# Router logits as one turned 128x256 block, and the stage lists of four phases in another order

## The chip, the cores and the metric

The kernel runs on one core of a Trainium2 chip. The metric is the time of one execution on the device in microseconds (us), given as the median of three runs. The engines are called PE or TensorE (matrix products and transposes), DVE or VectorE, ACT or ScalarE, POOL or GpSimd, and SP or SyncE, whose queue issues most of the transfers (DMAs). Each engine works through its own queue in order, and waits where an operand is not ready.

## The reference

The input is `x` of 32 sequences by 128 tokens by 128 features, with a context of the same shape. Two decoder layers follow each other, and each adds three parts to `x`: attention of 16 heads of 8 features, cross-attention to the context, and a mixture of 16 experts of which each token uses four. The routing of the first layer is

```python
scores = jax.nn.sigmoid(x2d @ router_weight.T)
sc = scores + e_bias[None, :]
group_scores = jnp.sum(jax.lax.top_k(sc.reshape(T, G, E // G), 2)[0], axis=-1)
_, gidx = jax.lax.top_k(group_scores, TG)
masked = jnp.where(smask > 0, sc, 0.0)
_, tidx = jax.lax.top_k(masked, K)
tw = jnp.take_along_axis(scores, tidx, axis=1)
```

and in the second layer the logits `x @ gate_w.T` are used without a sigmoid, with a softmax over the chosen four. The result per token is a row of 16 combine weights, zero for the experts not chosen; each expert's output is multiplied by its weight and summed.

## The kernel before

The 4096 tokens are 32 batches of 128; a group `g` is four batches (512 tokens, `GT`), and there are eight groups. A routing set `n` is two groups, eight batches (`NBR`), so each layer has four sets. Activations are kept per group in two forms: by token (`x[g]`, 128 tokens by 4 batches by 128 features) and, after normalisation (`xn`) and a turn on PE (`by_feature`, which transposes each batch), by feature (`hs[g]`, 128 features by 512 tokens), as matrix products need them.

**Routing.** `routing(n)` makes the logits of a set. For each of its eight batches one matmul takes the 128x128 block of `hs` as the stationary operand and the 16 router columns `W["r"]` as the moving one, so that token ends up on the partition: `lg` is 128 tokens by 8 batches by 16 experts in PSUM. A matmul in f32 is two records in the trace. `route` is a generator that turns the logits into combine weights, some steps at a time (`choose`, `chosen`): in the first layer it starts with a sigmoid on ACT (`route_groups`, with a load of ACT's tables before and after it), in the second with a copy on DVE (`route_softmax`, and `route` of the row tables). Routing happens eight times: set 0 of the first layer in `first_layers`, sets 1 to 3 in `mixture_layer`; three sets of the second layer in `second_layers`, the last (called n3) in `last_layer`.

**Send.** `send(n)` turns the combine weights to expert-by-token: eight transposes of 128x16 into `pct`, two ACT copies of 16x512 into slots of the ring `xn` (two buffers, shared with the normalised activations), and two DMAs into the DRAM tensors `combined`. Later `fetch` reads them back, each expert's row spread over 128 partitions (`share`). Send happens five times: four sets of the first layer and set 1 of the second.

**Gathered rows.** Sets 0, 2 and 3 of the second layer do not multiply all tokens with all experts. `placed` computes where each (token, choice) goes; `way_out` scatters rows into `rows_in` with 32 indirect DMAs on POOL per set; SP reads quads of four 128-row tiles (`rows_of`: one `rows` transfer, then four `row_weights`); PE multiplies them (`rows_turned`, `rows_up`, `rows_down`); `way_back` gathers the results with 32 indirect DMAs per set into `back` (three buffers), and `added` adds them to `x` on DVE.

**Order.** There are four phases: `first_layers` (0 to about 578 us: attention and cross-attention of layer one), `mixture_layer` (to about 798), `second_layers` (attention and cross-attention of layer two, to about 1062) and `last_layer`. Each is one call of `steps` with a list of stages. An entry `(stage, at, every, count, behind...)` runs the stage first at step `at` and then every `every` steps, `count` times. Within a step the stages of the list are written out in the order of the list; after each piece of one of them, one piece of a `between` stage is filled in, the first of the `between` list that still has pieces; what is left over is written at the end of the step. A stage named behind an entry waits in the list for that one. `first_layers` and `last_layer` are written by hand from the first step (`as_written=0`) and `second_layers` from step 8: there the order of the lists is the order in each engine's queue (in `last_layer` in SP's too). `mixture_layer` is left to the Tile scheduler, which takes the list as a priority.

In `first_layers` group `g`'s attention runs with four steps per group: `project` makes queries and keys with the rotary products, `turn` transposes them, `average` and `finish_` divide the weighted sums and apply the output projection (DVE `aT`, PE `proj`). `biased` adds the output bias to `x` on POOL. `second_layers` does the same with feature maps (`totals` makes `pS` and `fsums`, `finish` the projection).

## Time and profile before

| | |
|---|---|
| median of three runs | 1350.46 us (1350.32 to 1351.31) |
| the profiled execution | 1348.26 us, of which the span is 1346.2 us |
| mean granted clock of PE | 0.971 |
| instructions | 27567 |
| PE busy | 1236.1 us (92%) |
| DVE, ACT, POOL busy | 857.6, 581.2, 531.4 us |
| `logits` on PE | 128 records, 11.3 + 3.8 us |
| `pct` on PE, its copy on ACT | 40 records, 5.3 us; 10 copies of 16x512, 5.5 us |
| HBM traffic | 99.34 MB read, 27.85 MB written |

A row of a timeline has the start in us, the length in us, the engine, the line of the kernel, the operation, the output and input tiles with their shapes, the number of records, and in brackets the idle time before it with what ended it. A row of stretches has, for each stretch, its length, then the busy time and number of instructions of PE, of PE's weight load, of DVE, ACT and POOL, then the granted clock of PE (1.00 is full), the mean busy share of the DMA engines and GB/s. In the view of slices each digit is the busy share of one fortieth of the span in tenths. Records of PE overlap: the step from one start to the next is what one occupies.

### The profile page before, as it was taken

How to read it: one execution, taken by the hardware profiler on the slowest of the kernel's cores; microseconds unless marked ns; L12 is line 12 of the kernel's file. 1: busy time of each engine (PE TensorE's matmuls, PEld its weight loads, DVE VectorE, ACT ScalarE, POOL GpSimd, SP SyncE). 2: the span in 40 equal slices, each digit the busy share in tenths (PEclk: the TensorE clock that was granted, in tenths of full speed). 3: DMA queues.
4: the chain of work that ended last, by engine and by line, in shares of the span. 5: the costliest groups of instructions: out<-in, count | busy, mean ns of one | idle time of the engine just before them, and what ended most of it. 6: DMA issues, size and time to landing. Idle time of an engine off the chain costs nothing. (4 is left out here: it accounts for less than half of the span.)

```text
span 1346.2 us, 27567 instructions
## 1 busy us (share of the span) xinstructions
PE 1236.1 (92%) x10753; PEld 835.9 (62%) x10753; DVE 857.6 (64%) x2295; ACT 581.2 (43%) x856; POOL 531.4 (39%) x715
## 2 busy tenths in 40 slices
PE   7689999999999999699999989999987889989995
PEld 6357767777777777544344446666664457767753
DVE  5746867677768675376866536787877575225463
ACT  4445445454555433232332234665654424433331
POOL 6244243445351222132100015455527653746654
PEclk9789999999999999899999999999998899999998
DMA  9401321121211111363262320000000488999933
GB/s 327 126 1 33 101 65 34 33 51 31 50 29 37 34 33 33 75 145 85 43 127 61 66 100 2 2 2 2 2 2 25 144 256 272 306 296 287 305 120 93
DMA packets 89673, 129.07 MB, mean 96 GB/s; under 512 B 9888, under 2 KB 63776, under 8 KB 88128
## 3 DMA queue, kind: packets, MB, share of 16 engines
q1 hardware_dynamic: 76768, 102.59, 27.2%
q0 software_dynamic: 6144, 12.60, 3.0%
q10 hardware_dynamic: 6624, 12.05, 2.4%
q8 instruction: 87, 1.43, 0.4%
q14 instruction: 50, 0.41, 0.1%
HBM read 99.34 MB, written 27.85 MB: 94 GB/s over the span
## 5 line engine op out<-in xcount | busy, mean ns | idle before, releaser
L1307 ACT ACTIVATE e<-scores 128x1024 f32<-128x1024 f32 x128 | 124.1, 1021 | 67.3 <-PE scores L977 67.2
L977 PE MATMUL y<-sg,wide 128*128 128x512 f32 x224 | 119.3, 621 | 15.1 <-DVE sg L2268 8.0
L2245 POOL DMA_INDIRECT back<-rows_out,place x96 | 91.2, 950 | 58.7 <-DVE x L2256 31.1
L1145 POOL TENSOR_SCALAR xn<-x,mv,r 128x128 f32<-128x128 f32 x78 | 67.4, 870 | 91.3 <-PE pxn L1154 82.7
L1927 ACT ACTIVATE sg<-pg 128x512 f32<-128x512 f32 x72 | 43.0, 597 | 118.9 <-PE pg L977 110.0
L1561 ACT ACTIVATE e<-xscores 128x1024 f32<-128x1024 f32 x64 | 62.0, 1021 | 67.7 <-PE xscores L977 67.7
L1322 DVE STREAM_TRANSPOSE by_token<-sums 128x512 f32<-128x512 f32 x64 | 45.3, 707 | 71.0 <-PE sums L977 70.9
L1928 DVE TENSOR_TENSOR sg<-sg,pu 128x512 f32<-128x512 f32 x72 | 49.3, 685 | 60.7 <-PE pu L977 58.1
L1116 POOL TENSOR_SCALAR r<-mv 128x4 f32<-128x4 f32 x46 | 13.2, 286 | 189.2 <-DVE mv L1135 189.2
L977 PE MATMUL scores<-qb,k 32*128 32x512 f32 x512 | 75.2, 658 | 13.4 <-ACT e L1307 7.0
L1116 POOL TENSOR_SCALAR r2x<-mv 128x2 f32<-128x2 f32 x16 | 3.8, 235 | 195.3 <-DVE mv L1135 195.3
L977 PE MATMUL pg<-hx,wide 128*128 128x512 f32 x152 | 78.0, 595 | 0.0
L977 PEld LDWEIGHTS y<-sg,wide 128*128 128x128 f32 x224 | 36.6, 191 | 66.3 <-DVE sg L1930 36.3
L977 PE MATMUL pu<-hx,wide 128*128 128x512 f32 x152 | 77.7, 593 | 0.0
L977 PE MATMUL sums<-e,v 128*32 128x128 f32 x2048 | 72.7, 284 | 0.7 <-ACT e L1307 0.7
L977 PE MATMUL po<-e,v 128*64 128x128 f32 x1024 | 66.2, 280 | 4.3 <-DVE v L1575 4.2
L2230 DVE TENSOR_TENSOR sgrows<-sgrows,pu 128x512 f32<-128x512 f32 x36 | 24.7, 687 | 70.6 <-PE pu L977 61.2
L977 PEld LDWEIGHTS sums<-e,v 128*32 128x32 f32 x2048 | 56.7, 113 | 19.3 <-issue 4.9
L1609 ACT COPY av<-po 128x512 f32<-128x512 f32 x64 | 37.6, 587 | 71.2 <-PE po L977 70.4
L977 PE MATMUL po<-av,wide 128*128 128x256 f32 x256 | 60.0, 388 | 7.7 <-DVE av L1629 7.7
L977 PE MATMUL pqk<-h,wide 128*128 128x256 f32 x256 | 64.4, 397 | 1.1 <-ACT h L1157 1.1
L977 PEld LDWEIGHTS po<-e,v 128*64 128x64 f32 x1024 | 56.4, 139 | 12.8 <-issue 7.4
(326 smaller groups left out, 2974.0 us busy)
## 6 DMA issues: line engine op xcount, KB each, us to landing
row_weights<-in_w1f_dram SPq DMA_DIRECT2D x144, 192.0 KB, 4.0
factor<-factors SPq DMA_DIRECT2D x64, 256.0 KB, 4.4
share<-combined SPq DMA_DIRECT2D x32, 512.0 KB, 14.2
rows_in<-in_few SPq DMA_DIRECT2D x36, 256.0 KB, 4.2
rows<-rows_in SPq DMA_DIRECT2D x36, 256.0 KB, 4.0
rows_out<-yrows ACTq DMA_DIRECT2D x36, 256.0 KB, 4.5
share<-combined SPq DMA_DIRECT2D x8, 1024.0 KB, 5.4
wide<-in_w1f_dram SPq DMA_DIRECT2D x1, 3272.0 KB
```

What stands on the lines that cost most here:

```text
L977: last[0] = nc.tensor.matmul(*args, **kw)
L1116: nc.gpsimd.tensor_scalar(t, src, add, None, ALU.add)
L1145: eng.tensor_scalar(n[:, b, :], x[g][:, b, :], mv[:, b, 0:1], r[:, b : b + 1], ALU.subtract, ALU.mult)
L1307: nc.scalar.activation(e[-1], ps[:, bass.ts(n, 2)].rearrange("p c i s -> p (c i) s"), AF.Exp, scale=scale)
L1322: nc.vector.transpose(tt.rearrange("p i t r -> p (i t r)"), po.rearrange("p i s -> p (i s)"))
L1561: nc.scalar.activation(e[-1], ps[:, n].rearrange("p r c s -> p (r c) s"), AF.Exp, scale=scale)
L1609: nc.scalar.copy(avs[w][n][:, :, bass.ts(b, S)], po)
L1927: nc.scalar.activation(sg, pg, AF.Silu)
L1928: nc.vector.tensor_tensor(sg, sg, pu, ALU.mult)
L2230: nc.vector.tensor_tensor(sg, sg, pu, ALU.mult)
L2245: nc.gpsimd.indirect_dma_start(out=outs[n, u][:, k], out_offset=None, in_=rows_out[n], in_offset=bass.IndirectOffsetOnAxis(ap=places[n][:, ...
```

## The change

`logits` replaces the matmuls of all four routings. The stationary operand is now 32 columns wide (the 16 router columns and the 16 that lie next to them in the weight tile, whose results are not read), and each of four matmuls has 256 tokens as the moving operand and writes to one quarter of the 128 PSUM partitions. ACT copies the 128x256 result to SBUF, into a slot of the ring `xn` (in `last_layer` of a tile `turned`), and two 128x128 transposes on PE bring the tokens back to the partitions. The reader takes them in another order through `by_chunk`. `send` transposes a set's 128x128 combine weights at once, copies them in one ACT instruction, and stores each half with a DMA of 64 rows of 512 bytes. In all four phases the entries of the stage lists are permuted, and some start at another step.

```diff
...
+    def wider(self, name, n):
+a = self.spans[name][0]
+return self.tile[:, a : a + n]
+
...
     (weights, 4, 1, NU),
-    (lambda k: xvalues(2 * k), (5, 12), 2, EARLY - 1),
     (lambda w: xproject("k", w + EARLY), 8 + 2 * EARLY, 2, NW - EARLY),
+    (lambda k: xvalues(2 * k), (5, 12), 2, EARLY - 1),
     (lambda k: xvalues(2 * k + 1), 11, 2, NW),
     (xfinish_a, 13, 2, NW),
-    (lambda g: average(g * GB + GB + 3), 12, 4, NG - 1),
     (turn_in, (1, 3, 9), 4, NG, scaled),
+    (lambda g: average(g * GB + GB + 3), 12, 4, NG - 1),
     (xturn, (8, 13), 4, NG, xscaled),
     (xweights, (9, 11), 1, NU),
+    of_four(average, 0, 5),
     (finish_, 12, 4, NG - 1),
...
     of_four(average, 2, 7),
-    of_four(average, 0, 5),
     (lambda _: average(3), 7, 1, 1),
     of_four(average, 1, 6),
-    (finish_first, 7, 1, 1),
     [
...
     (first(routing), 29, 1, 1),
+    (first(send), 39, 1, 1, choose),
     (turn, (3, 7, 11), 4, NG, head_norms),
-    (head_squares, (2, 5, 10), 4, NG, head_means),
-    (first(send), 40, 1, 1, choose),
+    (finish_first, 7, 1, 1),
     (xfinish_b, 13, 2, NW),
+    (head_squares, (2, 5, 10), 4, NG, head_means),
     (xaverage, (9, 11), 1, NU),
...
         (xfinish_c, 14, 2, NW),
+        (norms, (0, 1, 8, 12), 4, NG),
         (head_means, (2, 5, 10), 4, NG),
...
         (xscaled, (8, 13), 4, NG),
-        (norms, (0, 1, 8, 12), 4, NG),
         (xnorm, (7, 12), 4, NG, finish_first, finish_),
-        (biased, 3, 4, NG),
-        (lambda _: choose(0, 5), 30, 1, 11),
+        (biased, 1, 4, NG),
         (xnormalize, 12, 2, NW, xweights),
         (rnorm_, 22, 4, NBR // GB),
-        (filled, 15, 1, 12),
         (rscaled_, 23, 4, NBR // GB),
+        (lambda _: load_w0f(), 21, 1, 1),
         (lambda k: load_late(LATE[k]), (17, 18), 1, len(LATE)),
-        (lambda _: load_w0f(), 20, 1, 1),
+        (filled, 16, 1, 12),
+        (lambda _: choose(0, 5), 30, 1, 11),
     ],
...
+    def by_chunk(s):
+
+return s.rearrange("p (c j) e -> p c j e", j=2)
+
+    def logits(wk, r, sources, name):
+
+
+pl = sm([128, 2 * S], "logits")
+for c, rows in enumerate(quarters):
+    mm(pl[rows], lhsT=r, rhs=sources[c // 2][:, bass.ts(c % 2, 2 * S)], start=True, stop=True)
+t = wk.tile([128, GT], F32, name=name, bufs=2)[:, 0 : 2 * S]
+nc.scalar.copy(t, pl)
+pt = sm([128, 2, S], "plogits")
+for j in range(2):
+    nc.tensor.transpose(pt[:, j], t[:, bass.ts(j, S)], ident)
+return pt.rearrange("p j (c e) -> p c j e", c=4)[:, :, :, 0:E]
+
     def route_groups(lg, wk):
...
 s = wk.tile([128, NBR, E], F32, name="s", bufs=1)
-nc.scalar.activation(s, lg, AF.Sigmoid)
+nc.scalar.activation(by_chunk(s), lg, AF.Sigmoid)
 yield
...
 s = wk.tile([128, NBR, E], F32, name="s", bufs=1)
-nc.vector.tensor_copy(s, lg)
+nc.vector.tensor_copy(by_chunk(s), lg)
 yield
...
 def routing(wk, n):
-    lg = sm([128, NBR, E], "logits")
-    for i, g in enumerate(groups(n)):
-        for b in range(GB):
-            mm(lg[:, i * GB + b, :], lhsT=hs[g][:, bass.ts(b, S)], rhs=W["r"], start=True, stop=True)
+    lg = logits(wk, W.wider("r", 32), [hs[g] for g in groups(n)], "xn")
     choices[n] = route(lg, n)
...
     comb = combs.pop(n)
+    pt = sm([128, S], "pct")
+    nc.tensor.transpose(pt, comb.rearrange("p b e -> p (b e)"), ident)
+    cT = wk.tile([128, GT], F32, name="xn", bufs=2)[:, 0:S]
+    nc.scalar.copy(cT, pt)
     for i, g in enumerate(groups(n)):
-        pt = sm([E, GB, S], "pct")
-        for b in range(GB):
-            nc.tensor.transpose(pt[:, b, :], comb[:, i * GB + b, :], ident)
-        cT = wk.tile([E, GT], F32, name="xn", bufs=2)
-        nc.scalar.copy(cT, pt.rearrange("p b s -> p (b s)"))
         weights[g] = dram.tile([E, GT], F32, name="combined")
-        nc.sync.dma_start(out=weights[g], in_=cT)
+        dst = bass.AP(weights[g].tensor, weights[g].offset, [[S, GB], [GT, E], [1, S]])
+        nc.sync.dma_start(out=dst, in_=cT[bass.ts(i, GB * E), :])
...
+also = [(lambda k, more=stage: more(wk, k), *when) for stage, *when in more]
 steps(
-    (fetch, 0, 1, 1),
-    (lambda _: fetch(1), 0, 1, 1),
+    (lambda n: groups(norm, scaled)(n + 2), 3, 4, NR - 2),
+    also[0],
+    also[3],
+    also[5],
     (lambda _: groups(norm, scaled)(1), 0, 1, 1),
     (lambda _: groups(turn)(1), 0, 1, 1),
-    (lambda n: groups(norm, scaled)(n + 2), 3, 4, NR - 2),
     (lambda n: routing(n + 1), 0, 4, NR - 1),
-    (lambda n: stages[4](n + 1), 0, 4, NR - 1),
+    also[4],
     (lambda n: groups(turn)(n + 2), 3, 4, NR - 2),
     (lambda n: send(n + 1), 3, 4, NR - 1),
+    (lambda n: stages[4](n + 1), 0, 4, NR - 1),
+    (lambda _: fetch(1), 2, 1, 1),
     (lambda n: fetch(2 * n + 2), 3, 4, NR - 1),
-    (lambda n: fetch(2 * n + 3), 4, 4, NR - 1),
-    *((lambda k, more=stage: more(wk, k), *when) for stage, *when in more),
+    (lambda n: fetch(2 * n + 3), 3, 4, NR - 1),
+    (fetch, 0, 1, 1),
+    also[1],
     (experts, 0, 1, 2 * NG),
+    also[2],
 )
...
     s = edge.tile([128, NBR, E], F32, name="s", bufs=1)
-    nc.vector.tensor_copy(s, lg)
+    nc.vector.tensor_copy(by_chunk(s), lg)
     yield
...
 def routing(n):
-    lg = sm([128, NBR, E], "logits")
-    for i, g in enumerate(of_set(n)):
-        for b in range(GB):
-            mm(lg[:, i * GB + b, :], lhsT=hs[g][:, bass.ts(b, S)], rhs=W["r"], start=True, stop=True)
+    lg = logits(wk, W.wider("r", 32), [hs[g] for g in of_set(n)], "turned")
     choices[n] = tables.route(lg, n)
...
 steps(
-    fetch_at(5, 6),
     fetch_at(0, 0),
+    fetch_at(4, 3),
     fetch_at(1, 0),
+    fetch_at(5, 6),
     fetch_at(2, 0),
-    fetch_at(4, 3),
-    fetch_at(6, 9),
     (several(each(rows_of, quads), (0, 1)), 0, 1, 1),
-    fetch_at(3, 0),
-    (several(turn, of_set(n3)), 6, 1, 1),
     once(tables.owned, n2, 3),
+    (several(turn, of_set(n3)), 6, 1, 1),
+    fetch_at(3, 0),
+    fetch_at(6, 9),
     (each(rows_turned, quads), Q, 1, NQ),
-    once(routing, n3, 6),
     (ups, 0, 1, LAST),
...
     (each(rows_up, quads), Q, 1, NQ),
-    fetch_at(7, 16),
     once(tables.owned, n3, 12),
+    once(routing, n3, 6),
+    fetch_at(7, 16),
     (downs, 0, 1, LAST),
...
     between=[
-        once(several(norm, of_set(n3)), None, 3),
+        (each(added, batches(0)), 23, 1, NBR),
         once(tables.placed, n2, 1),
-        once(chosen, n3, 7),
-        (each(added, batches(n2)), 33, 1, NBR),
+        (each(added, batches(n3)), 42, 2, NBR),
+        once(several(norm, of_set(n3)), None, 3),
         (each(rows_of, quads[2:]), Q, 1, NQ - 2),
-        (each(tables.way_out, to_send(n2, 2)), 2, 1, 4),
-        (each(way_back, batches(n3)), 40, 2, NBR),
+        once(chosen, n3, 7),
         once(tables.placed, n3, 9),
-        once(chosen, n2, 0),
+        (each(tables.way_out, to_send(n3, 1)), 9, 1, NBR),
+        (each(tables.way_out, to_send(n2, 2)), 1, 1, 4),
         (each(way_back, batches(n2)), 29, 1, NBR),
+        once(chosen, n2, 0),
+        (each(added, batches(n2)), 32, 1, NBR),
+        (each(way_back, batches(n3)), END + 1, 2, NBR),
         once(several(scaled, of_set(n3)), None, 4),
-        (each(added, batches(0)), 24, 1, NBR),
         (each(way_back, batches(0)), 19, 1, NBR),
-        (each(tables.way_out, to_send(n3, 1)), 10, 1, NBR),
-        (each(added, batches(n3)), END + 4, 2, NBR),
     ],
...
 steps(
+    (finish, 9, 4, NG),
     (features_q, 3, 4, NG),
...
     (later(project), 5, 4, NG - 1),
-    (finish, 9, 4, NG),
+    (xvalues, 11, 4, NG),
     (later(turn), 6, 4, NG - 1),
     (lambda _: send(early, 1), 43, 1, 1),
-    of_four(xweights, 2, 14),
     of_four(xweights, 1, 13),
-    (first(rturn), 20, 4, 3 * R),
-    (xvalues, 11, 4, NG),
+    of_four(xweights, 2, 14),
+    (later(turn_in), 4, 4, NG - 1),
     of_four(xweights, 3, 15),
-    (xkey, 10, 4, NG),
     (xturn, 11, 4, NG, xscaled),
-    (later(turn_in), 4, 4, NG - 1),
+    (first(rturn), 20, 4, 3 * R),
+    (xkey, 10, 4, NG),
     (average, 5, 1, NU),
...
     (xaverage, 13, 1, NU),
-    (xfinish, 17, 4, NG),
-    (xproject, 11, 4, NG),
     (first(routing), (25, 33, 42), 1, 3),
     of_four(xweights, 0, 12),
+    (xfinish, 17, 4, NG),
+    (xproject, 11, 4, NG),
     between=[
+        (norm_, 0, 4, NG - 1),
         (xscaled, 11, 4, NG),
+        (lambda _: choose(1, 3), 34, 1, 6),
+        (first(rscaled), 19, 4, 3 * R, xturn),
+        (scaled_, 3, 4, NG - 1),
         (placed, 33, 1, 1),
-        (lambda _: choose(1, 3), 35, 1, 6),
-        (lambda i: tables.way_out(0, to_send[3 * i : 3 * i + 3]), 36, 1, 11),
         (xnorm, 10, 4, NG),
-        (lambda _: choose(0, 3), 26, 1, 6),
-        (first(rscaled), 19, 4, 3 * R, xturn),
-        (norm_, 0, 4, NG - 1),
+        (lambda _: choose(0, 3), 27, 1, 6),
+        (lambda i: tables.way_out(0, to_send[3 * i : 3 * i + 3]), 37, 1, 11),
         (first(rnorm), 18, 4, 3 * R),
-        (scaled_, 3, 4, NG - 1),
     ],
...
         mixture0,
-        ((l1_setup, 10, 1, 1), *((lambda _, k, i=i: stages[i](k), 11 + i, 1, 1) for i in range(5))),
+        ((l1_setup, 10, 1, 1), *((lambda _, k, i=i: stages[i](k), at, 1, 1) for i, at in enumerate((10, 10, 12, 14, 16)))),
     )
```

## The prediction, made before the changed kernel ran

> **What bounds the kernel now.** I read the page's busy times and slices first, to see which engine is full and where; then the same by stretches of time; then the timeline of TensorE around each place that the change touches.
>
> ```profile
> PE 1236.1 (92%) x10753; PEld 835.9 (62%) x10753; DVE 857.6 (64%) x2295; ACT 581.2 (43%) x856; POOL 531.4 (39%) x715
> ...
> PE   7689999999999999699999989999987889989995
> ...
> DMA  9401321121211111363262320000000488999933
> ```
>
> TensorE works 92% of the span, and the digits below 9 are where it waits: the start, about 540 to 580, about 1000 to 1060, and the last layer. The stretches say the same in us:
>
> ```profile
> 200.00:525.00 325.00, 323.43 (x3609) 248.18 (x3608) 239.79 (x609) 155.63 (x219) 115.72 (x164) 1.00 0.16 38
> ...
> 600.00:780.00 180.00, 177.76 (x483) 76.92 (x482) 116.77 (x289) 52.72 (x88) 15.82 (x20) 1.00 0.35 72
> 800.00:1000.00 200.00, 191.17 (x2590) 133.30 (x2582) 147.70 (x432) 119.05 (x166) 93.99 (x141) 1.00 0.03 13
> ...
> 1062.00:1300.00 238.00, 215.53 (x1266) 161.59 (x1267) 117.41 (x295) 89.14 (x148) 137.50 (x143) 0.96 0.85 274
> 1300.00:1346.00 46.00, 32.27 (x113) 17.75 (x111) 18.13 (x43) 9.48 (x16) 25.63 (x28) 0.90 0.28 82
> ```
>
> The first column after the length is TensorE. From 200 to 525 and from 600 to 780 it is the bound at full clock (1.00): what it no longer does there comes off the span. From 1062 on the DMA share (0.85) stands beside it, and after 1300 the end hangs on POOL's gathers. The places themselves:
>
> ```profile
> 389.00 1.03 PE L977 MATMUL pqk<-h,wide 128*128 128x256 f32 x4
> ...
> 392.02 1.85 PE L977 MATMUL logits<-wide,hx 128*128 128x16 f32 x16
> 393.72 0.69 PE L977 MATMUL proj<-wide,o 128*128 128x128 f32 x4
> 394.35 1.08 PE L977 MATMUL xsums<-e,ones_by 128*32 128x128 f32 x32
> 395.36 0.88 PE L977 MATMUL po<-e,v 128*64 128x128 f32 x12
> ```
> ```profile
> 543.28 1.04 PE L1894 MATMUL pct<-in_few,comb 128*16 128x128 f32 x8
> 544.60 1.08 PE L977 MATMUL xsums<-e,ones_by 128*32 128x128 f32 x32 [0.28 <-ACT xn L1896]
> 548.27 3.76 PE L977 MATMUL po<-e,v 128*64 128x128 f32 x32 [2.60 <-DVE v L1575]
> ```
> ```profile
> 577.98 0.71 PE L977 MATMUL proj<-wide,o 128*128 128x128 f32 x4 [0.53 <-ACT o L1644]
> ```
>
> From one start to the next, 16 logits records hold TensorE 1.70 us (392.02 to 393.72).
>
> **Routing (8 times).** Removed: 1.70 us. Added on TensorE: four matmuls of 256 columns into four column quarters, two records each, and two transposes. The trace has no quarter matmul of 256 columns. Bounds: 32 quarter records of 128 columns take 1.01 us (394.35 to 395.36), so eight of twice the width take 0.50; run one after another they cost as the full-width 256-column records do, (389.86-389.00)/4 = 0.215 each, 1.72. I take 0.50, since the nearest row has the same shape of stationary tile and differs only in width. Transposes: eight take about 1.0 us here (the pct rows, and eight pxn in 1.04), so two 0.25. New total 0.75, serial 1.97.
> The Trainium skill ("TensorE: Matmul & The Clock Gate", section "Why this matters for your kernels") gives 2.38x for three column tiles where the row above shows more than three-fold overlap (32 records in 1.01 us, against about 0.12 each for the transposes); by it the four matmuls would be an estimated 0.72 us, and eight routings 1.8 us dearer than I count.
>
> Between the two halves now stands a ScalarE copy of 128x256. The nearest row is the 384 ns ScalarE pass over 128x256, which stopped TensorE 0.53 us at 577.98. Where the transposes follow the logits directly (first layers, second layers, last layer) I charge 0.53, at least 0 and at most one exponential of 1.02 more. In the mixture layer the scheduler puts another 512-column matmul (0.86 us from start to start) in between, which covers 0.53; without that cover 1.6 us come back over three routings. The sigmoid or copy after it reads the same 128x128 values in another order; its 0.28 to 0.29 us are off TensorE's path. The copy lies in ScalarE's idle time (52.72 busy of 180).
> The Trainium skill ("TensorEngine Tiling (Array Packing)", "PSUM Bottleneck") speaks against the change here: tiling quickens TensorE but not the copy out of PSUM, which can become the limit; by it all eight would stall, 1.6 us more than I count.
> So a routing saves 1.70-0.75 = 0.95 covered, 0.42 stalled.
>
> **Send (5 times).** Eight transposes (543.28 to 544.60 less the wait of 0.28: 1.04; 0.96 at 1054.99) become one, 0.12: saves 0.84 where TensorE is full. Two ScalarE copies of 574 ns become one (128x128 rows: 267 ns). The two DMAs stay two, 64 rows of 512 B instead of 16 of 2 KB, 32 KB each; SyncE's queue is otherwise in the same order but for one send that moves ahead of one factor transfer, two issues of about 0.5 us in a queue that idles there.
>
> **Stage by stage.**
> First layers, start. The turn of group 0 moves ahead of the output projection, where TensorE waited 3.26 and 0.76 us for DVE's aT (61.49, 63.04), so the scores come up to 3.5 us sooner; but the next chain (x, its norm, POOL's and ScalarE's parts, then pqk at 72.19) runs through the same projection. POOL's bias add (1.27 us) moves ahead of the rotary adds: at the start it may delay them by 1.27, later it falls into POOL's idle 6.3 to 7.6 us before them. Range -3.5 to +1.3; I take -0.5, the part of ScalarE's work that certainly leaves that chain. Routing(0) at 392: -0.42. The send at 543: 0, because TensorE then waits 2.60 for VectorE's v, behind a factor transfer that does not move; what is late next is the same transfer. The stop of 7.29 us at 571.26 for a factor is as it was.
>
> Mixture layer (TensorE 177.76 of 180): three routings 2.85, three sends 2.52. At its end TensorE stands 0.85 (795.06, VectorE's sg) with a 512-column matmul behind it that now goes before: -0.85. Eight transposes of rotated keys (0.86) leave the full stretch for a place where TensorE idled 0.78; their two ScalarE copies and a POOL pass then end about when the next stage needs them: -0.7 to +1, I take -0.35. The other moves here (fetches, the second layer's first stages at steps 10, 10, 12, 14, 16) permute work inside the full stretch, and SyncE's queue keeps its order: 0. Sum -6.6 (-4 to -8.5).
>
> Second layers. Routing -0.42. The output projection moves ahead of pS and qkv (3.6 us sooner). It needs aT (reciprocal 0.96, multiply 0.29). In the first group that ends at 823.9 and TensorE arrives at 822.5: +1.4. In four later groups (847, 875, 904, 933) aT is there 0.4 to 0.6 us before the new slot: 0. VectorE: an add (0.28) and four Max passes (0.41) move ahead of a norm that TensorE already waits 1.90 for: +0.7. Near 1034, where TensorE waits 3.62 for VectorE's norm, two statistics passes go into earlier idle time: -0.8. POOL's scatter of set 0 starts a step later, so three calls (1.26 apart) no longer stand before the context norm, for which TensorE waited 0.18, 1.10 and 0.33: at most -1.6, I take -0.65, less than half, since the exponentials stop it 2.12 soon after. Last routing and send at 1053: the copies are shorter, -0.85. The second routing lies before a wait of 2.02 for VectorE: 0. Sum -0.6 (-4 to +4).
>
> Last layer. Those three scatter calls are made up at the end, where 8 calls in a row become 11:
>
> ```profile
> 1072.33 0.95 POOL L2138 DMA_INDIRECT rows_in<-wide,place  x1 [0.30 <-issue]
> ```
> ```profile
> 1074.57 0.32 SPq L2195 DMA_DIRECT2D rows<-rows_in  x1
> 1075.65 2.89 SPq L2209 DMA_DIRECT2D row_weights<-in_w1f_dram  x4
> ```
> ```profile
> 1087.83 1.05 PE L977 MATMUL pg<-hrows,row_weights 128*128 128x128 f32 x8
> ```
>
> Set 0 is scattered about 4 us later (3 x 1.26), SyncE's first row transfer waits for it, and all its weight transfers queue behind. Landing 6.9 us after issue (median there), the first weights come at 1078.5+6.9+4 = 1089.4 against a need at 1087.8; from 1094.76 on the queue waits for free buffers anyway. Range 0 to +4, I take +1. Routing(n3) -0.42; its VectorE copy comes one chunk later, but the placement keeps its place in VectorE's order, so the 4.54 wait for set n3's rows at 1186.40 stays. The adds of returned rows move one or two steps earlier. The end does not hang on them: the last quad's results (pyrows 1289.43, out at 1291.24) release 32 POOL gathers, 1294.15 to 1333.9, and TensorE idles 7.99 us for those. 0.
>
> Sum: -0.5 -0.42 -6.6 -0.6 -0.42 +1.0 = -7.5. The profiled execution took 1348.26 (span 1346.2, 2.06 around it), 2.2 under the median of 1350.46. From its own time 1340.8; on the scale of the medians **1343**.
>
> **Rivals.**
> Only half: quarters run serially. A routing then costs 1.97, or 2.50 with the stall: 3 x -0.27 and 3 x -0.80 turn my +4.1 of routings into -3.2, about 7.3 worse: 1350, no change. For it: the 512-column rows at full width show no overlap. Against: the 32 quarter records in 1.01.
> More: the start passes on its 3.5 and the second layers their 4: -7.5-3.0-3.4, 1336.6. For it: both waits stand in the trace. Against: each has a second chain at nearly the same time.
> Slower: the moved projection. It has only about 0.5 us of slack to aT in the later groups, and pS, qkv and all behind stand in TensorE's queue. If VectorE (147.70 busy of 200) reaches the reciprocal some 2 us later than before, TensorE waits 1.5 us in each of the other seven groups, +10.5, and the sum is +3: 1353.5. It decides at about 1.5 us of lateness. For it: VectorE is backlogged around 1000. Against: in most groups it waited 0.2 to 1.6 us for fsums, so it is on time.
>
> **How the numbers follow.** Two medians of this kernel tell apart about 0.2%, 2.7 us. Forecast (-3 to -11) 0.58, more 0.14, half or none 0.12, slower 0.16 (the projection 0.10, the late weights with an uncovered copy 0.06). Faster 0.72, same 0.12, slower 0.16. The range drops about 1 in 10 on each side: from the "more" case, 1336, to the slower one, 1353; the forecast's own is 1339 to 1347.
>
> **What would show it.** Right: PE busy lower by about 11 us; four quarter logits matmuls within 0.6 us; 600 to 780 still full with the mixture's end about 7 us sooner; rows<-rows_in of set 0 no more than 4 us later against the end of the second layers. Wrong: quarter records 0.2 us apart one by one; aT waits in the later groups; TensorE waiting for row_weights near 1085 to 1100.

## The result, and the profile after

The changed kernel took 1344.17 us (median of 11 executions, 1338.39 to 1348.84); the kernel before, on the same chip and between them, 1354.32 us (11 executions, 1347.78 to 1359.7). The ratio is 0.9928, with a 95% interval of 0.9903 to 0.9952: 9.8 us less, between 6.5 and 13.1. The forecast was a gain of 7.5 us, and its time 1343.0. Two slow executions of the kernel before, 1465.17 us at a granted clock of 0.832 and 1365.74 us, are left out of every comparison below.

The two profiles shown are further from this than the kernels are. The profiled execution of the changed kernel took 1345.81 us (span 1344.0), 2.45 us less than that of the kernel before; but that of before, with 1348.26, lies some 6 us under the median of its own executions, and its granted clock of 0.971 is above their mean. So below I read places and waits from the pair of profiles, and totals from the medians.

From the page of the changed kernel, its busy times and the slices:

```profile
PE 1225.4 (91%) x10670; PEld 821.1 (61%) x10670; DVE 853.2 (63%) x2295; ACT 580.1 (43%) x859; POOL 531.8 (40%) x715
...
PE   7689999999999999689999989999987789989995
...
PEclk9889999999999999789999999999989899989997
DMA  9401322111111111363253220000000378999933
```

TensorE is busy 10.7 us less (1236.1 before), close to the 11 that were announced, and its slices keep their shape. Of the stretches, in the columns explained with the profile before, those that answer to the ones shown there:

```profile
200.00:525.00 325.00, 322.74 (x3545) 247.10 (x3546) 234.94 (x600) 155.02 (x218) 109.79 (x159) 1.00 0.15 38
...
600.00:780.00 180.00, 177.82 (x458) 74.28 (x457) 120.50 (x298) 52.13 (x89) 16.38 (x21) 1.00 0.34 72
...
800.00:1000.00 200.00, 189.04 (x2559) 129.65 (x2551) 147.54 (x430) 117.48 (x165) 94.08 (x141) 0.99 0.01 3
...
1062.00:1300.00 238.00, 215.35 (x1269) 160.22 (x1270) 120.65 (x302) 90.64 (x151) 144.76 (x150) 0.97 0.84 276
1300.00:1344.00 44.00, 28.55 (x104) 16.11 (x102) 15.27 (x38) 8.28 (x14) 23.98 (x25) 0.82 0.28 83
```

The mixture layer (600 to 780) is as full as before: what left TensorE there was followed by other work at once. From 800 to 1000 TensorE is busy 2.1 us less in the same 200 us, with waits that were not there. Where the mixture layer ends, from its last matmul to the second layer's first positive keys (pkphi), before and then in the changed kernel:

```profile
795.06 1.12 PE L977 MATMUL y<-sg,wide 128*128 128x512 f32 x2 [0.85 <-DVE sg L1928]
796.92 0.66 PE L1945 MATMUL pyt<-in_few,y 128*128 128x128 f32 x4 [0.73 <-ACT y L1942]
...
803.01 0.50 PE L977 MATMUL pkphi<-feat,y 32*128 32x128 f32 x8 [1.66 <-ACT qphi L2468]
```
```profile
789.18 2.11 PE L981 MATMUL y<-sg,wide 128*128 128x512 f32 x4
792.02 0.66 PE L1963 MATMUL pyt<-in_few,y 128*128 128x128 f32 x4 [0.73 <-ACT y L1960]
...
799.45 0.50 PE L981 MATMUL pkphi<-feat,y 32*128 32x128 f32 x8 [1.65 <-ACT qphi L2489]
```

The wait of 0.85 us is gone, and from the last turned result (pyt) to the first positive keys it is 7.43 us instead of 6.09.

The new operations on TensorE's timeline, one routing of the first layers, one of the mixture layer and one send:

```profile
386.86 0.64 PE L981 MATMUL logits<-hx,wide 128*32 128x256 f32 x8
388.04 0.44 PE L1779 MATMUL plogits<-in_few,xn 128*128 128x128 f32 x2 [0.54 <-ACT xn L1776]
388.31 0.61 PE L981 MATMUL proj<-wide,o 128*128 128x128 f32 x4
...
621.60 0.27 PE L1910 MATMUL pct<-in_few,comb 128*128 128x128 f32 x1
621.71 1.02 PE L981 MATMUL pg<-hx,wide 128*128 128x512 f32 x2
...
637.43 0.64 PE L981 MATMUL logits<-hx,wide 128*32 128x256 f32 x8
638.00 1.13 PE L981 MATMUL pg<-hx,wide 128*128 128x512 f32 x2
638.96 0.38 PE L1779 MATMUL plogits<-in_few,xn 128*128 128x128 f32 x2
639.18 1.02 PE L981 MATMUL pu<-hx,wide 128*128 128x512 f32 x2
```

Eight quarter records occupy TensorE 0.57 us from start to start (637.43 to 638.00), the two turns 0.22 to 0.27, a send's turn 0.11. In the mixture layer the 512-column matmul at 638.00 stands between the halves and there is no wait; at 388.04 TensorE waits 0.54 us for the ScalarE copy. Where a factor ends the first layers:

```profile
543.28 1.84 PE L981 MATMUL po<-e,v 128*64 128x128 f32 x16 [3.71 <-DVE v L1579]
546.32 1.98 PE L981 MATMUL po<-e,v 128*64 128x128 f32 x16 [1.20 <-DVE v L1579]
...
568.72 3.78 PE L981 MATMUL po<-av,wide 128*128 128x256 f32 x8 [7.48 <-DVE av L1633]
573.80 3.78 PE L981 MATMUL po<-av,wide 128*128 128x256 f32 x8 [1.30 <-DVE av L1633]
...
578.12 0.71 PE L981 MATMUL proj<-wide,o 128*128 128x128 f32 x4 [0.53 <-ACT o L1648]
```

The wait for VectorE's v, 2.60 us before, is 4.91 now in two parts. The eight records at 573.80 ran at a granted clock of 0.50; those of before took 1.99 us at a clock of 1.00:

```profile
575.45 1.99 PE L977 MATMUL po<-av,wide 128*128 128x256 f32 x8 [0.41 <-DVE av L1629]
```

And the last layer's first rows and weights, on the queue of SyncE and on TensorE:

```profile
1079.57 0.32 SPq L2216 DMA_DIRECT2D rows<-rows_in  x1
1080.66 2.89 SPq L2230 DMA_DIRECT2D row_weights<-in_w1f_dram  x4
```
```profile
1089.20 1.05 PE L981 MATMUL pg<-hrows,row_weights 128*128 128x128 f32 x8
```

The rows go out 5.0 us later than before, their weights too, and TensorE starts the first matmul with them 1.37 later (1087.83 before) and shows no wait for weights: it does the layer's own matmuls meanwhile.

### The profile page after: what moved, and what is told of

The parts are those of the page before. It is cut to its first block, busy times and chain, and to the rows that moved or that the text cites. A ratio compares the mean times of both kernels' runs of the same rounds, so it can differ in the third digit from the quotient of the medians.

```text
span 1344.0 us, 27393 instructions
## 1 busy us (share of the span) xinstructions
PE 1225.4 (91%) x10670; PEld 821.1 (61%) x10670; DVE 853.2 (63%) x2295; ACT 580.1 (43%) x859; POOL 531.8 (40%) x715
## 4 chain that ended last, share of the span: by engine, by line
PE 63%; DVE 14%; DMA 8%; POOL 5%; ACT 4%; issue 3%; SPq 1%; POOLq 0%; DVEq 0%; ACTq 0%
PE pqk L981 7%; PE po L981 7%; PE pg L981 6%; PE pu L981 6%; PE y L981 5%; PE scores L981 4%; PE xscores L981 4%; PE pval L981 3%; PE sums L981 3%; DMA factor<-factors 3%; DMA row_weights<-in_w1f_dram 2%; PE proj L981 2%; PE pyrows L981 2%; POOL back L2266 2%; PE pS L981 2%
```

## The experiments

Theory A at the start: the cheaper logits and sends carry the gain by the price of each removed record, and the stage lists together give nothing. Against it: the lists carry the gain, or part of it, with the second rival that some of the lists give back what others win. To hold kernels against each other I use, beside the ratios, the phases of their profiles: the time from one fixed instruction on TensorE to another. A phase of a single execution scatters by 1 to 5 us, the long last one by 8, so only differences that repeat over several profiles count. "Before" below is the kernel before, measured among the others on the same chip: runs 1, 2, 4 and 7 form one series, 5, 6, 8 and 9 a second, 3, 10, 11 and 12 a third. The ratios are those on record; they differ from the quotient of the two medians by up to 0.002 (run 3: 0.9896 and 0.9916), so differences of that size say nothing. A diff is against the changed kernel, in run 5 against the kernel before and in run 10 against run 8.

**1. The values alone.** The new logits and sends, with all four stage lists and the steps of the second layer's first stages as before.

```diff
...
-(first(send), 39, 1, 1, choose),
 (turn, (3, 7, 11), 4, NG, head_norms),
-(finish_first, 7, 1, 1),
...
+(first(send), 40, 1, 1, choose),
...
```

> The matmuls, copies and transposes of the change, with all four stage lists as before. Theory A (TensorE's saved work carries the gain): about -5.4 us in the mixture layer and -1.7 elsewhere, 7 us faster than before (ratio 0.995), and the mixture layer shorter by 5 us. Theory B (the lists carry it): 3 us faster or less (0.998 or more).

Measured 1344.13 us against 1354.84, ratio 0.992 (0.9891 to 0.9949). The whole gain is there without a single list, and it is more than the 0.995 of theory A, which lies just outside the interval.

**2. The lists alone.** The lists and steps of the change, with the old logits (16 matmuls of 16 columns) and the old sends (eight turns, two copies).

```diff
...
-lg = logits(wk, W.wider("r", 32), [hs[g] for g in groups(n)], "xn")
+lg = sm([128, NBR, E], "logits")
+for i, g in enumerate(groups(n)):
+    for b in range(GB):
+        mm(lg[:, i * GB + b, :], lhsT=hs[g][:, bass.ts(b, S)], rhs=W["r"], start=True, stop=True)
...
```

> The four stage lists of the change, with the router matmuls and the send as before. Theory A: 1 to 3 us faster than before (0.998 to 0.999), since the start's 4.7 us are lost again at the factor transfers near 570 and the second layers get 4 us longer. Theory B: 5 to 7 us faster (0.995).

Measured 1358.31 us, ratio 1.0023 (0.9995 to 1.0051): no gain, and rather a loss of up to 7 us. The interval leaves out both theories' values; that the lists do not carry the gain, the core of theory A, stands, but the small gain it gave them is not there. Its profile is no clean picture of the lists: the mixture layer takes 217.78 us from its first turned group to its last turned result, and 9.86 us of that, from 587.61 on, ran at a granted clock of 0.52.

**3. The new logits without the new sends.** All lists as before, and the send as before.

```diff
...
-pt = sm([128, S], "pct")
-nc.tensor.transpose(pt, comb.rearrange("p b e -> p (b e)"), ident)
...
+pt = sm([E, GB, S], "pct")
+for b in range(GB):
+    nc.tensor.transpose(pt[:, b, :], comb[:, i * GB + b, :], ident)
...
```

> All lists as before, the weights turned and sent as before (eight turns, two copies); only the logits in column quarters and turned. Theory A (each removed matmul counts where TensorE is full): three routings of the mixture layer 0.91 each from the rows of after (1.70 less 0.57 less 0.22), 2.7; five others 0.3 to 0.4 each where no other wait stands behind them, 1.2 to 2: 4 to 5 us below before, ratio 0.9965. The rest of the 9 to 10 us of the values alone would then be the sends (3 x 0.76 = 2.3 in the mixture layer, up to 1 at the last send), which leaves 2 us without a place. Rival (the stall for ScalarE's copy eats the gain outside the mixture layer): 2.7 us, 0.998. Rival (the logits carry nearly all of it, since the matmuls behind them come at a higher granted clock): 7 us or more, 0.995 or below.

Measured 1343.43 us (9 executions) against 1354.86, ratio 0.9896 (0.9861 to 0.9931): 9 to 19 us, not the 4 to 5 of theory A, and in the range of the rival with the higher clock. Place by place, though, the price is the announced one: from the first turned group of the mixture layer to its last turned result the profile of before needs 214.95 us (581.97 to 796.92) and this one 212.05 (581.27 to 793.32): 2.90 less for three routings. With the sends as well (run 1) it is 4.87 less. So in the layer where TensorE is full each removed record counts, and the total is larger than the phases show. Part of that lies in the pair of profiles: that of before is one of its quick executions, and the profiled one here (1344.92) is only 3.3 us below it. What goes with the rest is the clock: over all three series the 91 compared executions of the kernel before have a mean granted clock of 0.9656, the 120 of the kernels with the new logits 0.9676 (standard errors 0.0004 and 0.0003), and within one kernel an execution is about 1.0 us longer for each 0.001 that its clock is lower. That would be 2 us; in this series alone, with 0.9691 against 0.9644, it would be more than 4. Why the clock differs was not tested, so the rival's mechanism is not shown, and what remains here, 2 to 5 us, is about the half width of the interval.

**4. The first layers' list of before in the changed kernel.**

```diff
...
+(finish_first, 7, 1, 1),
 [
     (lambda w: xproject("q", w), (8, 11), 2, NW),
     (project, (1, 4, 9), 4, NG, norms),
...
-(biased, 1, 4, NG),
+(biased, 3, 4, NG),
...
```

> The changed kernel with the list of the first layers as before. Theory A: the 4.7 us gained at the start end at the wait for the factor transfers near 570, so the mixture layer starts at the same time as in the changed kernel, and the time differs by 0 to +1 us. Theory B: they pass on to the end, and this is 4 to 5 us slower than the changed kernel.

Measured 1348.09 us, ratio 0.9953 (0.9925 to 0.9981): some 3.4 us above the changed kernel, which lies between the two theories, and the interval (3.8 us to each side) leaves both open. The profiles agree in direction. The first xsums (the sums of the cross-attention's exponentials) after the second turn, at 109.30 us before, comes at 108.84 to 110.07 in the four profiles with the list of before, and at 104.59 to 107.57 in the ten with the list of the change: 3.7 us earlier in the mean. Two places of TensorE before:

```profile
72.19 6.14 PE L977 MATMUL pqk<-h,wide 128*128 128x256 f32 x16 [1.08 <-ACT h L1157]
...
83.48 3.39 PE L977 MATMUL xscores<-qk 64*128 64x128 f32 x32
```

and what the changed kernel's TensorE does there:

```profile
58.57 0.44 PE L1491 MATMUL pturn<-in_few,y 128*128 128x128 f32 x2 [1.30 <-DVE y L1478]
...
62.31 0.49 PE L981 MATMUL proj<-in_fast,aT 128*128 128x128 f32 x2 [1.07 <-DVE aT L1333]
...
67.25 0.45 PE L1158 MATMUL pxn<-in_few,xn 128*128 128x128 f32 x1 [3.01 <-DVE xn L1149]
...
69.85 6.66 PE L981 MATMUL pqk<-h,wide 128*128 128x256 f32 x16 [0.68 <-ACT h L1161]
...
80.73 2.06 PE L981 MATMUL xscores<-qk 64*128 64x128 f32 x32
```

pqk starts 2.34 us sooner (72.19 before). VectorE's k copy (0.77 us) now runs ahead of the addition of x, where it stood among the statistics before; POOL's norm call starts at 65.37 instead of 67.30. The run takes back the whole list, so that the moved k copy brings the 2.34 is read from VectorE's queue and not tested alone. And the 32 xscores records that took 3.39 us at 83.48 before, at a granted clock of 0.57, take 2.06 here at 1.00: 1.3 us of the 4.68 are the clock. That part does not come with the list every time: in five of the nine profiles with the new logits and this list the 32 records take 3.19 to 3.59 us, and there xsums comes at 105.73 to 106.66.

**5. The values and the first layers' list,** the other three as before.

```diff
...
-(finish_first, 7, 1, 1),
 [
...
 (turn, (3, 7, 11), 4, NG, head_norms),
+(finish_first, 7, 1, 1),
...
```

> The matmuls, copies and turns of the change with the first layers' list of the change; the mixture, second layers' and last layer's lists as before. Theory A (the cheaper routings and sends carry the gain; of the lists only the first layers' one helps, about 3.4 us, and the other three give it back): about 3 us below the values alone, so a ratio of 0.989 to 0.990, some 1340.5, below both kernels shown. Rival (the lists work only together, the first layers' list helps because the later lists are there): as the values alone, 0.992, or above.

Measured 1340.58 us against 1350.41, ratio 0.9911 (0.988 to 0.9942). That lies between the two expectations (0.989 to 0.990 and 0.992), and the interval doesn't tell it from the values alone.

**6. The second layers' list of before in the changed kernel.**

```diff
...
-(lambda _: choose(0, 3), 27, 1, 6),
+(lambda _: choose(0, 3), 26, 1, 6),
...
+(later(turn_in), 4, 4, NG - 1),
 (average, 5, 1, NU),
...
```

> The changed kernel with the second layers' list of before. Theory A: the second layers' list costs the most of what the later lists give back; the trace of after shows +1.5 at the first group's output projection, 1.8 us more of waiting at 980 and 1.1 new at 1017, so this run is 3 to 4 us below the changed kernel, ratio 0.990. Rival (those waits only take the place of others; the loss lies in the mixture layer or in the last layer): as the changed kernel, 0.9925 to 0.9935.

Measured 1339.5 us, ratio 0.9908 (0.9882 to 0.9934), where theory A had 0.990 and the changed kernel stands at 0.9928: in its direction, and not outside the scatter. Its profile does not show the gain: from the first positive keys to the last output projection it has 264.06 us, against 263.25 and 262.27 in two profiles of the changed kernel, with a granted clock of 0.97 from 800 to 1000, where that of run 11 has 1.00.

**7. One entry of it: choose(0, 3) back at step 26.** In the changed kernel ScalarE takes the exponential `parts` (L2092) of this entry ahead of e and hq.

```diff
...
-(lambda _: choose(0, 3), 27, 1, 6),
+(lambda _: choose(0, 3), 26, 1, 6),
...
```

> The changed kernel with one entry of the second layers' list back at its step: choose(0, 3) at 26 and not at 27. If the exponential of the combine weights, now queued on ScalarE ahead of the exponentials and the hq copy at 978, makes the wait of 2.38 us at 980.61, that wait goes back to about 0.6 and the kernel is 2 to 3 us faster than the changed one. Rival: VectorE's backlog before the sb at 1003.89 takes it up, and the end of the second layers moves by less than 0.5.

Measured 1343.14 us, ratio 0.9924 (0.9898 to 0.9951). The wait went, as the profile says, and the total can't tell 2 us: from the first positive keys to the last output projection this profile has 260.00 us against 263.25 and 262.27 in two profiles of the changed kernel; but run 10, which keeps the wait, has 260.09.

**8. The mixture layer's list of before in the changed kernel,** with the second layer's first stages one step apart again.

```diff
...
-(lambda n: fetch(2 * n + 3), 3, 4, NR - 1),
-(fetch, 0, 1, 1),
-also[1],
+(lambda n: fetch(2 * n + 3), 4, 4, NR - 1),
+*((lambda k, more=stage: more(wk, k), *when) for stage, *when in more),
 (experts, 0, 1, 2 * NG),
-also[2],
...
```

> The changed kernel with the mixture layer's list of before, and the second layer's first stages one step apart again. The prediction gave this list 1.2 us of gain (0.85 for the last 512-column matmul put ahead of a wait, 0.35 for the turned rotated keys), so the run would be 1.2 us above the changed kernel, 0.9935. The trace of after says 1.3 us lost between the last turned result and the first positive keys, against 0.85 gained: 0 to 0.5 below. Rival (it is this list that gives back the start's gain): 3 us below, 0.990.

Measured 1346.63 us, ratio 0.9959 (0.9934 to 0.9985): a loss of 4 us against the changed kernel's ratio, where the expectation had one of 1.2 at most and its rival a gain. In its profile the mixture layer is no longer than in the others; the second layers are, with 264.43 us from the first positive keys to the last output projection. Runs 10 and 11 take this up.

**9. The last layer's list of before in the changed kernel.**

```diff
...
-(each(added, batches(n3)), 42, 2, NBR),
...
-(each(way_back, batches(n3)), END + 1, 2, NBR),
+(each(way_back, batches(n3)), 40, 2, NBR),
...
+(each(added, batches(n3)), END + 4, 2, NBR),
...
```

> The changed kernel with the last layer's list of before. The prediction gave it +1.0 for later weights; the trace of after shows no wait of TensorE for these weights, so 0: as the changed kernel, 0.9925 to 0.993. Rival (weights or the way back are late after all): 1 to 4 us below, 0.990 to 0.992.

Measured 1341.57 us (10 executions), ratio 0.9945 (0.9914 to 0.9976); the interval holds both the changed kernel's ratio and the rival's smaller gains (0.992). The profile is sharper than the ratio at one place, the tail, which run 12 shows.

**10. The mixture layer's list of before, the steps of the change.** As run 8, with the steps 10, 10, 12, 14, 16.

```diff
...
-*((lambda _, k, i=i: stages[i](k), 11 + i, 1, 1) for i in range(5))
+*((lambda _, k, i=i: stages[i](k), at, 1, 1) for i, at in enumerate((10, 10, 12, 14, 16)))
...
```

> The changed kernel with the mixture layer's list of before, but the second layer's first stages at the steps of the change (10, 10, 12, 14, 16). If the list's order carries the 4 us that the run with both undone lost: 0.996, as that run. If the steps of these stages carry them: 0.993, as the changed kernel beside it. If neither is real: 0.993 again, and the first of the two runs was scatter; then this run's profile has the mixture layer as long as in the others (216 to 219 us from its first turned group to the first positive keys).

Measured 1343.93 us against 1354.86, ratio 0.9936 (0.9904 to 0.9968), beside 0.9929 for the changed kernel in the same series, where the medians are 1343.93 and 1345.71. The list's order carries no 4 us. The phase from the first turned group to the first positive keys (215.72 us) is no longer than in the others, and neither was that of run 8 (216.25). The two differ in the steps alone, and the steps decide how the layer ends: run 8 has the wait of 0.85 us of before, 210.16 to the last turned result and 6.09 from there to the first positive keys; this run has no such wait, 208.30 and 7.42. Whether the steps also cost what run 8 lost in total, these runs don't decide: the two were measured in different series.

**11. The changed kernel again,** as the control of its series; no edit.

> The changed kernel itself once more, as the control beside the three others of this call, whose differences are near the scatter between calls. All theories: 0.9928 as first measured, within 0.003; some 9 to 10 us under before.

Measured 1345.71 us (1342.2 to 1349.97, 12 executions) against 1354.86, ratio 0.9929 (0.9902 to 0.9956): the first result once more.

**12. The values with the first layers' and the mixture layer's lists;** the second layers' and the last layer's lists as before.

```diff
...
+(later(turn_in), 4, 4, NG - 1),
 (average, 5, 1, NU),
...
+(each(added, batches(n3)), END + 4, 2, NBR),
...
```

> The matmuls, copies and turns of the change with the first layers' and the mixture layer's lists of the change; the second layers' and last layer's lists as before. Theory B (the mixture list gains 4 us by itself, as the run without it said): 4 us under the values with the first list alone, 0.988. Theory C (the mixture list gains nothing by itself; without it the run was slower because the other lists of the change were made for it, or by scatter): 0.991, as with the first list alone. The last layer's list of before should also show 1.2 to 1.6 us less between the last routed rows' matmul and the end (56.6 to 57.0 us in the three profiles that have it, 58.2 to 58.6 in those that have the other).

Measured 1338.91 us (1337.49 to 1341.67, 6 executions), ratio 0.9879 (0.9837 to 0.9922). The ratio to before takes theory B's value in its middle, and its interval holds theory C's too. Against the changed kernel of run 11, on the same chip in the same series, the answer is plainer: the slowest execution here (1341.67) is faster than the fastest there (1342.2), and the medians are 6.8 us apart. So the second layers' and the last layer's lists together cost time, some 4 to 7 us of it (the clock, 0.9688 here and 0.9668 there, goes with 2), and this version beats both kernels. Runs 6 and 9, which take back one of the two lists each, do not show it singly: 0.9908 and 0.9945 beside 0.9928. Two places of the profiles carry it. First the second layers' first group on TensorE, in run 11 (the changed kernel):

```profile
814.72 0.61 PE L1158 MATMUL pxn<-in_few,xn 128*128 128x128 f32 x4
...
817.45 0.49 PE L981 MATMUL proj<-in_w1a,aT 128*128 128x128 f32 x2 [0.54 <-DVE aT L2536]
...
823.84 0.77 PE L2470 MATMUL prot<-in_few,rot 128*128 128x128 f32 x5 [0.35 <-DVE frec L2534]
824.84 1.13 PE L981 MATMUL pk<-ctx,in_w1x 128*128 128x512 f32 x2 [0.24 <-ACT y L2472]
...
977.65 1.12 PE L981 MATMUL pq<-hq,in_w1x 128*128 128x512 f32 x2 [2.39 <-ACT hq L1161]
```

and in run 12, with the list of before:

```profile
816.08 0.60 PE L1158 MATMUL pxn<-in_few,xn 128*128 128x128 f32 x4
...
820.91 1.05 PE L981 MATMUL proj<-in_w1a,aT 128*128 128x128 f32 x8
...
824.70 1.12 PE L981 MATMUL pk<-ctx,in_w1x 128*128 128x512 f32 x2 [0.24 <-ACT y L2472]
...
976.10 1.12 PE L981 MATMUL pq<-hq,in_w1x 128*128 128x512 f32 x2 [0.56 <-ACT hq L1161]
```

From pxn to pk it is 10.12 us there and 8.62 here: the projection ahead of pS costs 1.50. The wait for hq costs 1.83 (2.39 against 0.56). From the first positive keys to the last projection the sum is 262.27 against 258.80.

Then the tail, TensorE's last routed rows and its last wait, and POOL's gathers among them, in run 11:

```profile
1282.41 1.16 PE L981 MATMUL pyrows<-row_weights,sgrows 128*128 128x128 f32 x8 [0.85 <-DVE sgrows L2251]
...
1330.65 2.07 PE L981 MATMUL y<-sg,wide 128*128 128x512 f32 x2 [9.10 <-DVE sg L2289]
```
```profile
1289.65 1.42 POOL L2266 DMA_INDIRECT back<-rows_out,place  x1 [0.30 <-issue]
1295.12 1.29 POOL L2266 DMA_INDIRECT back<-rows_out,place  x1 [0.31 <-DMA back<-rows_out,place]
...
1300.54 1.31 POOL L2266 DMA_INDIRECT back<-rows_out,place  x1 [0.30 <-DMA back<-rows_out,place]
```

and in run 12:

```profile
1278.97 1.16 PE L981 MATMUL pyrows<-row_weights,sgrows 128*128 128x128 f32 x8 [0.85 <-DVE sgrows L2251]
...
1326.03 2.07 PE L981 MATMUL y<-sg,wide 128*128 128x512 f32 x2 [7.92 <-DVE sg L2289]
```

48.24 us from one to the other there, 47.06 here. Three of the gathers take 1.29 to 1.42 us; in run 12 none of the same gathers takes more than 0.98. Behind the last pyrows all eight profiles with the last layer's list of the change have three gathers of 1.28 to 1.42 us, and 57.9 to 58.6 us to the end of the span; the six with the list of before have none above 1.08 there, and 56.6 to 57.3. Ahead of the last pyrows single gathers of 1.25 to 1.46 us stand in profiles of both.

## Why the prediction was right, step by step

The class and the time were right (1344.17 in a range of 1336 to 1353, against 1343.0), and the main mechanism is shown: what TensorE no longer does in the full mixture layer comes off. But the middle of the sum is right partly by luck, because errors of both signs met in it. Of the signs named, PE busy (10.7 us less), the quarters (0.57 us) and the full stretch hold; the mixture layer's last turned result came 4.9 us sooner in the pair shown (792.02 against 796.92) and not about 7, and the rows of set 0 went out 4.4 us later against the end of the second layers and not at most 4.

- **Routing and send, the prices.** Nearly right. Quarters 0.50 announced, 0.57 measured from start to start, and 1.01 at 586.32, where the granted clock was 0.61; turns 0.25, and 0.22 to 0.28; the stall 0.53, and 0.54 (388.04), 0.55 (996.81) and 0.49 (1115.29), with 0.94 only at 1056.12; a send's turn 0.12, and 0.11. A stalled routing, put at 0.42, saves 0.25 to 0.39 from its first record to the one behind its turns (1.45 at 386.86 against 1.70), and nothing at 1056.12. So the rival with serial quarters (1.72) is out. The Trainium skill ("TensorE: Matmul & The Clock Gate", section "Why this matters for your kernels") gives 2.38x for three column tiles; here eight records over four quarters overlap about threefold (0.57 where they would take 1.72 one by one). Its warning in "TensorEngine Tiling (Array Packing)", section "PSUM Bottleneck", that the copy out of PSUM can become the limit, came true at five of the eight routings for about half a microsecond each, once 0.94, and not at the three of the mixture layer.
- **Mixture layer.** From the first turned group to the last turned result the routings save 2.90 (run 3; announced 2.85), routings and sends together 4.87 and 4.79 (runs 1 and 8; announced 5.37), and with the steps of the change 6.65 (runs 9 and 10). The prediction put the steps at 0 and counted the 0.85 at VectorE's sg and the 0.35 of the rotated keys apart from them; runs 8 and 10 show that both come with the steps. These five profiles and that of before begin the layer at full pace. The seven others, whose first quarter records take 0.85 to 1.08 us instead of 0.64, save 2.1 to 5.5. The rotated keys' turns, put at -0.35, cost: from the last turned result to the first positive keys the changed kernel takes 7.43 us against 6.09, with waits of 0.34 and 0.68 in it. That is 1.34 more for 0.86 less in the full stretch, so +0.5; with the 0.85 the steps gain 0.4 to 0.5 us.
- **Start, the step that was mis-sized: -0.5 taken, -4.68 measured** at 109.3, of which 2.3 came through the chain that I called a second limit at nearly the same time and 1.3 through the clock. I had refused the gain because x's norm runs through the same projection. I hadn't followed VectorE's queue, where the k copy moved out of the middle of the statistics, nor asked at what clock the records behind the wait would run.
- **The send at 543 and the stop at the factor, at 0.** Here half of the start's gain is lost again. The send moved to 531; its eight turns and their wait, 1.32 us, had been the cover of the wait for v, and the second factor's multiplication came 1.81 us after the end of the first one (0.97 before): 4.91 of wait against 2.60, 2.3 of 5.5 given back. I named the work that hides, but not that the wait grows when the hidden work goes and TensorE comes sooner. In the profile shown the rest went at the last factor, 0.9 in a longer wait (1.30 against 0.41) and 1.8 in the eight records behind it at half pace (3.78 against 1.99): the mixture layer starts at 582.11 against 581.97. Over the nine profiles with the new logits and this list it starts at 579.50 to 582.26, in the three with the list of before at 581.27 to 584.47: 1.9 us stay in the mean.
- **Second layers: -0.6 taken, a loss measured.** With the new logits the six profiles with the list of the change take 260.09 to 264.43 us from the first positive keys to the last projection, the five with the list of before 258.80 to 264.06: 1.8 more in the mean, with ranges that overlap. Two parts repeat in every profile. The projection ahead of pS costs 1.50 (10.12 to 10.14 against 8.61 or 8.62 from pxn to pk), as the announced +1.4. And the wait for hq is 2.38 to 2.40 against 0.56: what failed is an edit that I did not cost at all, choose(0, 3) a step later, which puts an exponential that waits for VectorE ahead of hq in ScalarE's queue, 1.8 us; with that entry alone put back (run 7) the wait is 0.56. The statistics passes went the announced way (3.62 to 2.83). The context norm, put at -0.65, did not: its three waits sum to 1.61 before and to 2.04 in the changed kernel. A new wait of 1.13 for VectorE's sb (1017.93) was not seen either. The moved projection did not hurt in the later groups: that rival is out.
- **Last layer.** The weights came later as announced, and no wait for them shows where +1.0 was put: TensorE had other matmuls. The tail was put at 0 and cost 1.2 to 1.4.
- **The sum.** What the traces show is 5.3 in the mixture layer (4.8 by the values, 0.5 by the steps), 0.9 for the four routings behind it and 0.8 for the last send, about 1.9 of the start, and against it 1.8 to 3.3 in the second layers and 1.4 in the tail: 4 to 6 us. Measured are 9.8, with 6.5 as the lower end. Some 2 us go with the higher granted clock (run 3). What the others are is not settled. One stretch is 4 us shorter in the changed kernel, from the last projection of the second layers to the last pyrows (222.93 and 223.65 us against 227.37), but over all profiles it lies between 220.17 and 228.14 with either list of the last layer, so it cannot be put down to the change. The forecast's 7.5 came out close because the start was put too low, the second layers too well, and the clock not at all. And two medians are not told apart to 2.7 us, as the forecast had it: with 11 executions of each the interval is 6.6 us wide.

## What to carry to other kernels

Narrow results on TensorE are worth turning round: with 32-wide stationary tiles in the four column quarters and a long moving operand, the matmuls overlapped about threefold here, and the price is a copy and two turns; TensorE did not wait for the copy where another matmul stood between. Cost each reordered entry by the queue of every engine that it passes, and ask of each hidden piece of work what the wait will be without it: here the lists of two phases ate 4 to 7 us that the cheaper matmuls had won, and the version without them has the lowest ratio of all. Before a difference below 1% is sought in one pair of profiles, see where each lies among the executions of its own kernel.

## What the runs showed of the hardware that was not expected

- The executions of one and the same kernel scatter by 8 to 20 us where there are nine or more (before: 1344.95 to 1365.27), and most of it goes with the mean granted clock of TensorE: inside one kernel an execution is about 1.0 us longer for each 0.001 less of it, with a correlation between -0.7 and -0.9 inside the kernels of the first series. Which of the two brings the other, or whether both follow a third, was not tested.
- After a wait TensorE can run the next records at about half pace: 32 xscores records took 3.39 us at 83.48 before (granted clock 0.57) and 2.06 in the changed kernel (1.00), and in the changed kernel two 512-column records took 1.91 us at 1184.60 (0.50), soon after a wait of 4.47 us, where such a pair takes 1.02 elsewhere.
- POOL's gathers, 0.94 us each and one every 1.25 us, took 1.28 to 1.42 in three places behind the last pyrows in every profile with one order of the last layer's list, and at most 1.08 there with the other. Which engine or transfer lengthens them was not tested.
